# A new written order for the steps of a local attention, and the norm's bias product moved to GpSimd

## The chip, the cores and the metric

The kernel runs on one core of a Trainium2 chip. The metric is the time that the core takes for the whole kernel, in device microseconds (us). The engines are named as in the profile: PE is TensorE's matmul queue and PEld its weight loads, DVE is VectorE, ACT is ScalarE, POOL is GpSimd, SP is SyncE, which here only starts transfers.

## What is computed

The reference is a block of two layers on 16 sequences of 256 tokens with 128 features. Each layer has an attention-like part and a feed-forward-like part, each scaled and shifted per sequence (a modulation). The part that this change touches is the feed-forward place of the first layer, which is itself a small transformer of six layers with local attention in windows of 32 tokens:

```python
for i in range(DEPTH):                      # DEPTH = 6
    x = attn_layer(shift_tokens(x), Wqkv[i], q_scale[i], k_scale[i], Wo[i]) + x
    x = ffn_layer(shift_tokens(x), ln_g[i], ln_b[i], W1[i], b1[i], W2[i], b2[i]) + x

def attn_layer(x, Wqkv, qs, ksc, Wo):
    q, k, v = split(x @ Wqkv)               # 16 heads of 64
    q = l2norm(q) * qs;  k = l2norm(k) * ksc
    q = q * cos * scale + rotate_half(q) * sin * scale      # and k with 1 / scale
    out = local_attention(q, k, v)          # a window of 32 sees itself and the one before
    return out @ Wo

def ffn_layer(x, g, bln, W1, b1, W2, b2):
    mu = x.mean(-1);  var = ((x - mu) ** 2).mean(-1)
    xn = (x - mu) / sqrt(var + 1e-05) * g + bln
    a, gate = split(xn @ W1 + b1)
    return a * gelu(gate) @ W2 + b2
```

Ahead of it stands a full attention, behind it a state-space layer. Neither is changed.

## The kernel before

The kernel has three stages one after the other: `full_attention`, the class `Transformer` (the local attention), and `state_space`. `Transformer.run` handles two sequences at a time, which the code calls a group: eight groups in each of six layers, 48 in all. A group is cut into 172 small steps. Each step is a method whose name is the first letters of the step; the digits behind it say which part is meant, first the sequence of the pair (b, 0 or 1), then the half of its 256 tokens (t, 0 or 1), and where there is a third digit, a piece of the step. A `q` or `k` in the name says which of the two projections it is.

The steps of a group, with the engine of each:

- `P` (PE, line 594): projection of 128 tokens to q or k, into a two-bank tile of PSUM. `Q` (ACT, 604) squares it in two pieces, `N` (DVE, 620) multiplies it in two pieces by the sine table into `w`, `C` (DVE, 609) multiplies it by the cosine table into `u`. `R` (DVE, 631) sums the squares by head.
- `A` (POOL, 637): u + w. `MXS` (POOL, 640), `SQ` (ACT, 644) and `RR` (DVE, 647) make the reciprocal norm of the q and k of one sequence; `M` (POOL, 651) multiplies u by it.
- `T` (PE, 663): transposes of u. `E` (ACT, 679) copies them to SBUF.
- `X` (PE), `W` (ACT, 691) and `V` (SP, 696 and 697): the tokens of one sequence, and by two transfers a copy shifted by one window, in `xw`.
- `K` (ACT, 704) writes the mask into a PSUM tile, `S` (PE, 717) adds the scores to it, `MX` (DVE, 729) takes maxima, `SB` (DVE, 735) subtracts them, `EX` (ACT, 743) exponentiates, `SM` (DVE, 747 and 750) sums and inverts, `NR` (POOL, 754) scales, `TP` (DVE, 761) transposes.
- `G` (PE, 772): weights times tokens; `B` (ACT, 782) copies; `Y` (PE, 791): output product, in four pieces; `FADD` (DVE, 801) adds it to the tokens in `F`.
- The feed-forward part: `F1` (PE, 810) transposes, `F2` (DVE, 818 to 821) takes mean and variance, `F3` (POOL, 53) raises variance plus epsilon to the power -0.5, `FN` (DVE, 828) forms the bias -mean * rs, `F4` (ACT, 833) normalises, `F5` and `F6` turn it back, `FP` (PE, 863), `FE` (ACT, 867), `FM` (DVE, 873), `FY` (PE, 885) and `FF` (DVE, 898) are the two products with the gelu between them.

The string `ORDER` is the schedule. Each entry is a step and its lag: `TP11@2` means that in slot p the step `TP11` of group p - 2 is issued. `run` walks the whole list once in each slot, for 48 groups and three slots more. Every engine executes its instructions in the order in which they were issued, so the list sets the order on each engine. A slot therefore holds steps of up to four groups, and all 48 slots have the same order.

Three pools of buffers tie the engines together. The tag `two` has three PSUM tiles of two banks each; `P`, `T`, `K`/`S`, `G` (two) and `FP` all take one, 31 in each slot. The tag `one` has two single banks (`X`, `Y`, `F1`, `F5`, `FY`). In SBUF the tag `w` has four buffers, which the squares of `Q` and the products of `N` share, and `u` has seven. In the first slots of a layer `load` starts the transfers of the next layer's weights, and near its end `value_output` multiplies two weight matrices on PE.

Of the kernel before, what the change touches and what calls it, by code (L numbers as in the profile page):

```python
# [10 lines left out]
F32 = mybir.dt.float32  # L11
BF16 = mybir.dt.bfloat16
AF = mybir.ActivationFunctionType
ALU = mybir.AluOpType
# [3 lines left out]
P = 128  # L18
B, S, D = 16, 256, 128
NT = S // P  # L20
NTOK = B * S
G = 2
# [12 lines left out]
FF = int(D * 4 * 2 / 3)  # L35
# [422 lines left out]


ORDER = """  # L460
Pk01@0 Qk010@0 NR11@2 Mq00@1 TP11@2 Tq00@1 Eq00@1 Tk00@1 Aq11@1 Y03@2 Ek00@1 Aq10@1 NR10@2 Ck01@0
Nk010@0 Nk011@0 FADD0@2 TP10@2 Qk011@0 K00@1 G11@2 S00@1 MX00@1 SB00@1 FY@3 FF@3 MXS1@1 SQ1@1 B111@2
X1@1 Ak01@0 B110@2 G10@2 K01@1 RR1@1 S01@1 Mq11@1 Mq10@1 Mk10@1 EX00@1 SM00@1 MX01@1 Mk11@1 SB01@1
B100@2 Pq00@0 Rk01@0 B101@2 Qq000@0 Nq000@0 EX01@1 Pq01@0 Cq00@0 Y10@2 Qq010@0 Tq11@1 Nq001@0 Aq00@0
Y11@2 Qq011@0 Nq010@0 W1@1 Qq001@0 Cq01@0 NR00@1 Eq11@1 Nq011@0 Rq00@0 SM01@1 NR01@1 Tk11@1 Ek11@1
Rq01@0 Tk10@1 Ek10@1 Pk00@0 Ck00@0 X0@1 TP00@1 Tq10@1 Nk000@0 K11@1 S11@1 W0@1 Nk001@0 Eq10@1 MX11@1
SB11@1 Y12@2 Y13@2 V0@1 FADD1@2 Qk000@0 Qk001@0 Rk00@0 G00@1 K10@1 B000@1 S10@1 TP01@1 MXS0@0 Ak00@0
MX10@1 SB10@1 F1@2 B001@1 G01@1 Aq01@0 SQ0@0 RR0@0 B010@1 B011@1 Pk11@0 F2@2 F3@2 Pk10@0 Y00@1
EX11@1 Nk110@0 Nk111@0 FN@2 Ck11@0 Mk01@0 Ak11@0 Pq10@0 Nk100@0 Nk101@0 Qk110@0 V1@1 Ck10@0 Ak10@0
Qk111@0 Pq11@0 Mq01@0 Rk11@0 F4@2 Qk100@0 Qk101@0 Qq110@0 Qq111@0 Cq10@0 Qq100@0 Rk10@0 F5@2 EX10@1  # L470
Nq100@0 Nq110@0 Y01@1 Tk01@0 Qq101@0 F6@2 Y02@1 Nq101@0 Ek01@0 Nq111@0 Tq01@0 Eq01@0 Cq11@0 SM11@1
SM10@1 FP0@2 FE0@2 Rq11@0 FP1@2 FE1@2 Mk00@0 FM0@2 FP2@2 Rq10@0 FE2@2 FM1@2 FM2@2
"""


class Transformer:
# [335 lines left out]
    def F2(self, g):  # L812
        nc, n = self.c.nc, G * NT
        st = self.sb.tile([P, n, 6], F32, tag="fst", name="fst")
        g.mv = self.sb.tile([P, n, 2], F32, tag="fmv", name="fmv")
        g.rs = self.sb.tile([P, n], F32, tag="frs", name="frs")
        for i in range(n):
            nc.vector.bn_stats(st[:, i, :], g.f[:, i, :])
        for i in range(n):
            nc.vector.bn_aggr(g.mv[:, i, :], st[:, i, :])  # L820
        nc.vector.tensor_scalar_add(g.rs, g.mv[:, :, 1], EPS)

    def F3(self, g):
        inv_sqrt(self.c, g.rs, g.rs, [P, G * NT])

    def FN(self, g):
        g.nb = self.sb.tile([P, G * NT], F32, tag="fnb", name="fnb")
        self.c.nc.vector.scalar_tensor_tensor(g.nb, g.mv[:, :, 0], -1.0, g.rs, ALU.mult, ALU.mult)

    def F4(self, g):  # L830
        g.xn = self.sb.tile([P, G * NT, P], F32, tag="xn", name="xn", bufs=1)
# [682 lines left out]
```

## Time and profile before

| what | us |
|---|---|
| three timed runs, median (lowest to highest) | 4008.72 (4005.88 to 4009.32) |
| the profiled execution's own time | 4013.28 |
| its span, first to last instruction | 4011.4 |
| first `P` (line 594) starts | 443.1 |
| last `FF` (line 898) starts | 3452.8 |
| busy: PE, DVE, ACT, POOL | 3735.6, 3422.4, 2758.6, 2591.1 |
| mean granted TensorE clock over the span | 0.982 |

A row of the page's list of groups gives the line and engine, the operation, the output and inputs, the number of executions, the busy time and the mean duration in ns, and behind the bar the time for which the engine sat idle just before it and who ended that. In the timeline the columns are start, length, engine, line and operation, the number of instructions merged, and in square brackets the idle time before it and what ended it. In the timeline a length is that of the instruction; the next one of the same engine can start some hundredths of a us before its end.

### The profile page before, as it was taken

Reading aid. Unit: us, or ns where it says so; the run is one execution under the profiler, and the core shown is the slowest. Engines: PE = TensorE matmul, PEld = TensorE weight load, DVE = VectorE, ACT = ScalarE, POOL = GpSimd, SP = SyncE. Lnnn points to the kernel's source line nnn. Section 1 sums busy time; section 2 is a strip of 40 time slices with the busy share of each in tenths; the row PEclk is TensorE's granted clock in tenths of the full one; section 3 lists DMA queues with packets and bytes.
Section 4 is the critical chain, followed back from the end, with each engine's and each line's share of the span. In section 5 each row is a group of like instructions: output and inputs, shape, how many; then the busy total and the mean of one; then the engine's idle time right before and its main releaser. Section 6 shows DMA issues by size and latency. Waiting matters only on the chain.

```text
span 4011.4 us, 103903 instructions
## 1 busy us (share of the span) xinstructions
PE 3735.6 (93%) x45040; PEld 2202.1 (55%) x45040; DVE 3422.4 (85%) x4720; ACT 2758.6 (69%) x3962; POOL 2591.1 (65%) x1586
## 2 busy tenths in 40 slices
PE   7888789999999999999999999999999998599997
PEld 4444355555555555565655555555555555355554
DVE  4555489999999999999999999999999997299997
ACT  2555466777777777777767777677777676389995
POOL 1222477767767767767767677676676675188887
PEclk9999899999999999999999999999999999799999
DMA  0100001000010000100000000100000000134442
GB/s 24 35 7 4 1 6 34 4 7 4 6 34 4 7 7 4 34 7 4 7 10 28 7 4 6 34 4 6 7 4 7 6 4 7 53 99 114 117 110 74
DMA packets 84165, 94.42 MB, mean 24 GB/s; under 512 B 8872, under 2 KB 55804, under 8 KB 82940
## 3 DMA queue, kind: packets, MB, share of 16 engines
q1 hardware_dynamic: 83708, 87.76, 8.2%
q8 instruction: 355, 5.82, 0.6%
q14 instruction: 102, 0.84, 0.1%
HBM read 73.84 MB, written 2.62 MB: 19 GB/s over the span
## 4 chain that ended last, share of the span: by engine, by line
DVE 47%; PE 25%; POOL 11%; ACT 9%; issue 7%; DMA 0%; POOLq 0%; SPq 0%; DVEq 0%; ACTq 0%
DVE w L620 7%; DVE u L609 6%; DVE ss L631 6%; POOL u L637 6%; DVE pp L735 5%; DVE mx L729 5%; DVE sm L747 5%; PE pq L594 4%; PE y L1277 3%; PE pa L772 3%; DVE pT L761 3%; PE db L1261 2%; PE s L717 2%; ACT pp L743 2%; DVE act L873 2%
## 5 line engine op out<-in xcount | busy, mean ns | idle before, releaser
L637 POOL TENSOR_TENSOR u<-u,w 128x1024 f32<-128x1024 f32 x384 | 902.1, 2365 | 103.5 <-DVE u L609 63.0
L651 POOL TENSOR_TENSOR u<-u,r 128x1024 f32<-128x1024 f32 x384 | 722.5, 1903 | 282.7 <-DVE r L647 282.7
L594 PE MATMUL pq<-wqk,F 128*128 128x512 f32 x1536 | 731.6, 614 | 64.8 <-ACT at L782 30.8
L604 ACT ACTIVATE sq<-pq 128x512 f32<-128x512 f32 x768 | 427.7, 606 | 498.9 <-DVE w L620 258.5
L791 PE MATMUL py<-at,wvo 128*128 128x256 f32 x3072 | 743.3, 388 | 6.8 <-ACT at L782 6.3
L791 PEld LDWEIGHTS py<-at,wvo 128*128 128x128 f32 x3072 | 566.9, 191 | 132.8 <-issue 37.3
L620 DVE TENSOR_TENSOR w<-pq,sinl 128x512 f32<-128x512 f32 x768 | 493.4, 677 | 31.7 <-PE pq L594 24.0
L594 PEld LDWEIGHTS pq<-wqk,F 128*128 128x128 f32 x1536 | 275.7, 192 | 417.4 <-issue 234.0
L609 DVE TENSOR_TENSOR u<-pq,cosl 128x1024 f32<-128x1024 f32 x384 | 463.7, 1208 | 20.0 <-ACT sq L604 19.8
L631 DVE TENSOR_REDUCE ss<-sq 128x16 f32<-128x1024 f32 x384 | 459.1, 1196 | 3.3 <-ACT sq L604 1.9
L772 PE MATMUL pa<-pT,xw 32*128 32x512 f32 x3072 | 441.7, 616 | 19.9 <-ACT sq L604 16.3
L754 POOL TENSOR_TENSOR pp<-pp,sm 128x1024 f32<-128x1024 f32 x192 | 367.6, 1915 | 136.2 <-DVE sm L750 131.5
L782 ACT COPY at<-pa 128x1024 f32<-128x1024 f32 x384 | 367.9, 1010 | 52.6 <-PE pa L772 52.4
L717 PEld LDWEIGHTS s<-kT,qT 64*32 64x32 f32 x24576 | 259.6, 105 | 142.6 <-issue 77.5
L1267 DVE TENSOR_TENSOR_SCAN s<-da,db 128x512 f32<-128x512 f32 x256 | 301.1, 1207 | 24.8 <-PE db L1261 9.0
L717 PE MATMUL s<-kT,qT 64*32 64x64 f32 x24576 | 291.4, 227 | 27.3 <-ACT s L704 22.1
L729 DVE TENSOR_REDUCE mx<-s 128x16 f32<-128x1024 f32 x192 | 234.2, 1220 | 82.3 <-PE s L717 79.1
L704 ACT COPY s<-mask 128x1024 f32<-128x1024 f32 x192 | 195.3, 1017 | 155.4 <-DVE pp L735 151.8
L251 DVE TENSOR_REDUCE mx<-s 128x2 f32<-128x512 f32 x256 | 165.4, 687 | 157.8 <-PE sT L279 136.2
L663 PEld LDWEIGHTS pt<-ident,u 64*128 64x128 f32 x6144 | 217.5, 140 | 130.6 <-issue 108.4
L663 PE MATMUL pt<-ident,u 64*128 64x64 f32 x6144 | 257.8, 229 | 19.6 <-POOL u L651 6.6
L772 PEld LDWEIGHTS pa<-pT,xw 32*128 32x128 f32 x3072 | 171.6, 184 | 182.7 <-issue 105.3
(209 smaller groups left out, 6307.6 us busy)
## 6 DMA issues: line engine op xcount, KB each, us to landing
btd<-bc SPq DMA_DIRECT2D x72, 512.0 KB
bte<-bc SPq DMA_DIRECT2D x56, 256.0 KB
xw<-xw SPq DMA_DIRECT2D x96, 96.0 KB
wqk<-in_Wqk SPq DMA_DIRECT2D x6, 1024.0 KB
wv<-in_LWvT SPq DMA_DIRECT2D x6, 512.0 KB
wo<-in_Wo SPq DMA_DIRECT2D x6, 512.0 KB
xin<-in_x SPq DMA_DIRECT2D x8, 256.0 KB
out<-ot SPq DMA_DIRECT2D x8, 256.0 KB
```

Source lines behind the costliest of these rows:

```text
L594: nc.tensor.matmul(q.p[:, x], self.F[:, g.b0 + b, o : o + P], g.l.wqk[:, k, x, :], start=True, stop=True)
L604: self.c.nc.scalar.activation(q.sq[:, x], q.p[:, x], AF.Square)
L609: self.c.nc.vector.tensor_tensor(q.u.rearrange("p h x d -> p x h d"), q.p, g.l.cosl[:, t, k].unsqueeze(2).to_broadcast([P, 2, HEADS, DH // ...
L620: self.c.nc.vector.tensor_tensor(q.w[:, :, x], q.p[:, 1 - x], g.l.sinl[:, t, k, x, :].unsqueeze(1).to_broadcast([P, HEADS, DH // 2]), ALU. ...
L631: self.c.nc.vector.tensor_reduce(g.ss[b][:, t, k, :], q.sq.rearrange("p x h d -> p h x d"), AX.XY, ALU.add)
L637: self.c.nc.gpsimd.tensor_tensor(q.u, q.u, q.w, ALU.add)
L651: self.c.nc.gpsimd.tensor_tensor(uf, uf, g.r[b][:, t, k, :].unsqueeze(2).to_broadcast([P, HEADS, DH]), ALU.mult)
L663: self.c.nc.tensor.matmul(q.pt[:, r, j, :], uf[rs, j * P : (j + 1) * P], self.c.ident[rs, rs], is_transpose=True, start=(j == 0), stop=Tru ...
L717: nc.tensor.matmul(s[qs, e, j, :], qT[es, j, qs], kT[es, j, ks : ks + 2 * W], start=False, stop=True, skip_group_check=True,)
L729: self.c.nc.vector.tensor_reduce(g.mx[b, t], sf, AX.X, ALU.max)
L772: self.c.nc.tensor.matmul(g.pa[b, t, w // 2][:, w % 2, :], self.xw[b][qs, t, k, :], g.pT[b, t][qs, k, :], start=(k == 0), stop=(k == 1),)
L791: self.c.nc.tensor.matmul(g.py[b], g.l.wvo[:, h, :], self.at[:, h, :], start=(h == 0), stop=(h == HEADS - 1),)
```

## The change

`ORDER` is replaced by another list of the same steps. It starts at another point of the cycle, fifteen lags are changed (`NR10`, `NR11` and `TP10` have lag 1 and had 2; `FM1`, `FE2` and `FM2` have 3 and had 2; `X1`, `W1`, `V1` and `Y02` have 2 and had 1; `Rk10`, `Ak10`, `Tk01` and `Ek01` have 1 and had 0; `Aq11` has 0 and had 1), and the order within the slot is a new one throughout. The number of steps is the same.

The norm's bias is made in another way. `F2` makes -mean on DVE, once more a small instruction, and `FN` multiplies it by rs on GpSimd, where the power that makes rs is computed as well.

The code of the pools is not changed; which bank a tile gets follows from the order of issue.

```diff
 ORDER = """
-Pk01@0 Qk010@0 NR11@2 Mq00@1 TP11@2 Tq00@1 Eq00@1 Tk00@1 Aq11@1 Y03@2 Ek00@1 Aq10@1 NR10@2 Ck01@0
...
-SM10@1 FP0@2 FE0@2 Rq11@0 FP1@2 FE1@2 Mk00@0 FM0@2 FP2@2 Rq10@0 FE2@2 FM1@2 FM2@2
+Pq00@0 Rk10@1 Mq00@1 FM1@3 MXS1@1 Tk00@1 Ak10@1 FE2@3 FM2@3 SQ1@1 Nq000@0 Tq00@1 Nq001@0 Cq00@0
+TP11@2 Ek00@1 RR1@1 FY@3 Eq00@1 Mk11@1 FF@3 Aq10@1 K00@1 Aq00@0 Tk01@1 S00@1 Qq000@0 Mq10@1 Qq001@0
+Pk01@0 MX00@1 X1@2 Ek01@1 K01@1 Mq11@1 SB00@1 W1@2 S01@1 Nk010@0 Nk011@0 MX01@1 SB01@1 Ck01@0 V1@2
+Ak01@0 Pq01@0 EX00@1 Mk10@1 Qq010@0 Rq00@0 Y02@2 Y03@2 Qq011@0 Qk010@0 Qk011@0 G10@2 B101@2 Cq01@0
+Nq010@0 Nq011@0 X0@1 B100@2 FADD0@2 Aq01@0 G11@2 Rk01@0 SM00@1 EX01@1 B111@2 SM01@1 Pk00@0 NR00@1
+B110@2 Pq11@0 Tq10@1 Rq01@0 Qk000@0 Qk001@0 Qq110@0 Y10@2 Eq10@1 Nk000@0 Nk001@0 Ck00@0 Tk11@1 Y11@2
+Qq111@0 Nq110@0 Tq11@1 Ek11@1 Eq11@1 Tk10@1 Nq111@0 Cq11@0 TP00@1 Pk11@0 NR01@1 TP01@1 Ek10@1 Rk00@0
+Aq11@0 Y12@2 MXS0@0 Ck11@0 K11@1 S11@1 K10@1 S10@1 Nk110@0 Nk111@0 W0@1 V0@1 Ak11@0 Qk110@0 MX11@1
+SB11@1 Qk111@0 SQ0@0 MX10@1 Ak00@0 Y13@2 EX11@1 FADD1@2 G01@1 F1@2 SB10@1 B010@1 F2@2 B011@1 EX10@1
+F3@2 G00@1 B000@1 RR0@0 Rq11@0 Mq01@0 B001@1 SM11@1 Pq10@0 FN@2 Nq100@0 Pk10@0 Mk00@0 Qq100@0 SM10@1
+F4@2 Tq01@0 Nq101@0 NR10@1 Y00@1 Cq10@0 Eq01@0 Qk100@0 Rk11@0 F5@2 F6@2 Ck10@0 Qq101@0 Qk101@0 Y01@1
+Mk01@0 Rq10@0 FP0@2 FP1@2 Nk100@0 Nk101@0 FP2@2 FE0@2 NR11@1 TP10@1 FE1@2 FM0@2
 """
...
         nc.vector.tensor_scalar_add(g.rs, g.mv[:, :, 1], EPS)
+        g.nb = self.sb.tile([P, n], F32, tag="fnb", name="fnb")
+        nc.vector.tensor_scalar_mul(g.nb, g.mv[:, :, 0], -1.0)
...
     def FN(self, g):
-        g.nb = self.sb.tile([P, G * NT], F32, tag="fnb", name="fnb")
-        self.c.nc.vector.scalar_tensor_tensor(g.nb, g.mv[:, :, 0], -1.0, g.rs, ALU.mult, ALU.mult)
+        self.c.nc.gpsimd.tensor_tensor(g.nb, g.nb, g.rs, ALU.mult)
```

More of the change, by code (lines that the diff above doesn't have):

```diff
@@ L460 @@
 ORDER = """
-Pk01@0 Qk010@0 NR11@2 Mq00@1 TP11@2 Tq00@1 Eq00@1 Tk00@1 Aq11@1 Y03@2 Ek00@1 Aq10@1 NR10@2 Ck01@0
[L462 to L471, printed above, removed]
-SM10@1 FP0@2 FE0@2 Rq11@0 FP1@2 FE1@2 Mk00@0 FM0@2 FP2@2 Rq10@0 FE2@2 FM1@2 FM2@2
+Pq00@0 Rk10@1 Mq00@1 FM1@3 MXS1@1 Tk00@1 Ak10@1 FE2@3 FM2@3 SQ1@1 Nq000@0 Tq00@1 Nq001@0 Cq00@0
[10 more added lines that the diff above has]
+Mk01@0 Rq10@0 FP0@2 FP1@2 Nk100@0 Nk101@0 FP2@2 FE0@2 NR11@1 TP10@1 FE1@2 FM0@2
 """
```

## The prediction

> **What bounds the kernel now.** The page came first: its rows of busy tenths say where a stage is bound, and that the middle 30 slices are one regime.
>
> ```profile
> PE   7888789999999999999999999999999998599997
> DVE  4555489999999999999999999999999997299997
> ACT  2555466777777777777767777677777676389995
> POOL 1222477767767767767767677676676675188887
> ```
>
> From slice 6 to 33 PE and DVE are both at 9, ACT and POOL have room. The windows view puts figures to one stretch (us, then busy us of PE, PEld, DVE, ACT, POOL, then the granted clock):
>
> ```profile
> 1400.00:1800.00 400.00, 386.30 (x5588) 234.80 (x5587) 369.76 (x488) 284.22 (x373) 283.43 (x155) 1.00 0.05 13
> ```
>
> The clock is full there, so it explains nothing. Next is the timeline of DVE over one slot. The slot is a loop, so the same step comes again one period later: here `MX00`.
>
> ```profile
> 1600.37 1.22 DVE L729 TENSOR_REDUCE mx<-s 128x16 f32<-128x1024 f32 x1
> ...
> 1625.28 0.17 DVE L821 TENSOR_SCALAR frs<-fmv 128x4 f32<-128x4 f32 x1
> 1625.90 1.29 DVE L620 TENSOR_TENSOR w<-pq,sinl 128x512 f32<-128x512 f32 x2 [0.46 <-PE pq L594]
> 1627.11 1.35 DVE L828 SCALAR_TENSOR_TENSOR fnb<-fmv,frs 128x4 f32<-128x4 f32 x1
> ...
> 1650.85 1.25 DVE L761 STREAM_TRANSPOSE pT<-pp 128x1024 f32<-128x1024 f32 x1 [0.70 <-POOL pp L754]
> 1653.57 1.22 DVE L729 TENSOR_REDUCE mx<-s 128x16 f32<-128x1024 f32 x1 [1.47 <-PE s L717]
> ...
> 1656.27 1.98 DVE L898 SCALAR_TENSOR_TENSOR F<-fy,vec,F 64x256 f32<-64x256 f32 x4 [0.22 <-PE fy L885]
> ...
> 1659.56 1.22 DVE L747 TENSOR_REDUCE sm<-pp 128x16 f32<-128x1024 f32 x1 [0.72 <-ACT pp L743]
> ...
> 1661.10 1.23 DVE L729 TENSOR_REDUCE mx<-s 128x16 f32<-128x1024 f32 x1
> ```
>
> The period is 1661.10 - 1600.37 = 60.73 us. DVE waits five times in it: 0.46 + 0.70 + 1.47 + 0.22 + 0.72 = 3.57. Its work is the rest, 57.2. I check that from starts to next starts, since lengths overlap by some hundredths: 16 `N` at 0.60, 8 `C` at 1.13, 8 `R` at 1.12, 4 each of `MX` 1.25, `SB` 1.15, `SM` with its reciprocal 1.47, `TP` 1.16, then `FADD` 1.76, `F2` 1.31, two `RR` 1.0, `FN` 1.27, `FM` 1.97, `FF` 2.0: 57.1.
>
> PE in the same way, start to next start in stretches without a wait: `P` 14.0, `Y` 14.2, `G` 7.7, `S` 5.7, `T` 5.1, `FP` 5.3, `FY` 2.6, `X`, `F1` and `F5` 1.7: 56.3. So PE waits 4.4 of 60.7. POOL: 8 `A` at 2.32, 8 `M` at 1.86, 4 `NR` at 1.9, the rest 1.7: 42.8. ACT has 43 with its five table loads. Two engines have nearly the same work, and what is lost is waits of both on each other. A new order can win at most 60.7 - 56.3.
>
> Here the Trainium skill differs from the row. Its page "Perfetto Trace Analysis", section "Identifying the Most-Contended Engine", says that matmul busy time is no measure of PE's headroom and that the busy share of weight loads is one. That share is 234.8/400 = 59%; by it PE is no limit and the floor is DVE's 56. By starts PE needs 56.3. I use the starts; busy time (386.3/400 of 60.73, 58.6) would make PE the bound at 58.6, and I keep that as a rival.
>
> **The bias product.** `FN` leaves DVE: minus 1.27 a group (1627.11 to 1628.38 in the timeline above). `F2` gains one small instruction. The nearest row is its neighbour `frs`, the same kind and size, 0.17. A rule speaks against it: the page "SBUF — State Buffer", section "Who interferes with whom", says that a DVE operation with a scalar can take both ports when source and target are in SBUF, and that DVE and GpSimd then exclude each other for a whole instruction. By the rule the new instruction could wait for the power that `frs` has just released, 1.04 by its row; DVE would then save 0.1. By the row it saves 1.10. I take the row, because the new instruction is queued straight behind `frs` and starts before GpSimd can answer (the power starts 0.08 after `frs` ends). Both ends stay in the range: 0.1 to 1.1, or 5 to 52 us over 48 groups if nothing else bound.
>
> On POOL `FN` costs between 0.37 (the clamp `ss`, 128x64) and 1.04 (the power, 128x4); I take 0.6. It is queued behind one `M`. `F4` waits for it, but ACT has `Qq100` ahead of `F4`, which ends about 0.5 later than `FN` in the walk below, so it is hidden; with 1.04 it is just not late. Behind it on POOL stand `Mk00` and `NR10`; `NR10` waits for `SM10` anyway.
>
> **The order.** I read the instruction order and waits of the changed kernel, engine by engine, and walked one slot with the durations above. Each engine's order is the written one. New work is none: table loads are again two each for `SQ` and `EX` and one for `FE`.
>
> The first finding is a loop through POOL. `Nq010` takes the `w` buffer that `Ak01` reads. POOL reaches `Ak01` only after a run that begins when `RR1` ends on DVE: `Mk11`, `Aq10`, `Aq00`, `Mq10`, `Mq11`, `Ak01`.
>
> ```profile
> 1644.27 4.69 POOL L637 TENSOR_TENSOR u<-u,w 128x1024 f32<-128x1024 f32 x2
> ...
> 1658.98 3.76 POOL L651 TENSOR_TENSOR u<-u,r 128x1024 f32<-128x1024 f32 x2 [5.49 <-DVE r L647]
> ```
>
> The two POOL lines give 2.35 for an `A` and 1.88 for an `M`. The run is three of each, start to start 12.56, and with the step from `RR` to `M` (0.15) and back to DVE (0.04) 12.75. DVE has from `RR1` to `Nq010`: `FF` 2.0, `MX00` 1.25, `SB00` 1.15, two `N` 1.2, `MX01` 1.25, `SB01` 1.15, `Ck01` 1.13, `Rq00` 1.12, `Cq01` 1.13, together 11.4. So DVE waits 1.37 there, in each slot. All its other work is 56.0 - 11.4 = 44.6 (56.0 is 57.1 - 1.27 + 0.17). The loop is 44.6 + 12.75 = 57.35.
>
> The second is where PE meets it. `G11` takes the bank that `Nq011` frees; PE arrives about 1.1 early and waits. From there PE runs on: `Pk00` starts at 2.0 after `Nq011`, `Pq11` 3.7, `Y10` 6.2, `Y11` 8.6, `Pk11` 11.7, `Y12` 13.4, `S11` 15.15 to 16.75. DVE reaches `MX11` at 16.4: a wait of 0.35. `MX10`, `FADD1` and `F1` to `F2` fit within 0.15, `G00` waits 0.1 for `SB10`, `Pq10` ends 0.8 before `Nq100` wants it, `FP0` follows `F6` by 0.5, `FY` ends just as `FF` is due. Of the five waits of before, those for `P`, `EX` and `NR` are gone: `TP00` has its `NR` 5 us early, `SM00` its exponentials 9. The wait of `MX` shrinks from 1.47 to 0.35, that of `FF` to about 0.1, and 1.37 on the `w` buffer is new.
>
> Period: 57.35 + 0.35 + 0.05 = 57.75, against 60.73: 2.98 less.
>
> Moved transfers: `V0` and `V1` are two transfers each on SP. In the trace a copy `W` ends at 1611.70 and SP is through with the pair at 1613.8, so about 3 us to landing. The new order leaves 4.4 us (`V0` to `G01`) and 6.4 (`V1` to `G10`): hidden. If that cover went, PE would lose each us. The next layer's weights go to SP behind `V0`, for about 7 us, and `V1` comes over 30 later.
>
> "Banks given out by which is free first" is in no line of code: it can only have shaped the list, and is priced by the walk.
>
> **The sum.** From the first to the last `FN` lie 47 periods: 47 x 2.98 = 140. In the last layer `FF` has four more instructions of 0.48; before, those periods were 1.25 longer. Here 1.37 of DVE's wait covers them, leaving 0.56: 8 x 0.7 = 5 more. Filling and draining (147 us from the first `P` to the first `FN`, 18 after the last) I leave as they are: lags still end at 3; no row shows it, and I allow 10 either way. 4013.3 - 145 = 3868 for an execution like the profiled one, which was 4.6 above the median of the runs: **3864**.
>
> **Rivals.** (1) PE's busy time is its real need: the period stops at 58.6 to 59.5. For it: 97% busy. Against it: starts of `P`, `Y` and `FP` are even (0.43, 0.22, 0.43) and the waits between blocks visible. Time: 47 x (60.73 - 59.0) = 81, so about 3927.
> (2) The buffer wait doesn't bind, because POOL is early: PE's 56.3 and small waits give 56.9; 47 x 3.8 = 180, so 3829. Against it: three `M` and three `A` have the most even durations of all rows.
> (3) Slower: POOL's run starts late. `RR1` waits for `SQ1`, that for `MXS1`, which is queued behind `NR11` and `Mq00`. `RR1` has 3.1 of slack, the period 3.0; from 6.1 of POOL delay on, the kernel is slower, 47 us for each us. At 7.5 late: 4075. For it: POOL works off five instructions in a row there. Against it: it is idle before `Mk11` for 2.6 in my walk.
> (4) The list changes nothing, one wait for another: 4008.
>
> **Chances.** Forecast, period 57.2 to 58.4 (3840 to 3895): 0.60. Rival 1: 0.20. Rival 2: 0.07. Rival 3: 0.10. Rival 4: 0.03. Faster by over 0.2% (8 us, about what can be told from no change) is 0.87, slower 0.10. The range from 3832 to 3945 takes in the forecast, rival 1 up to 59.5 and the dearer bias product (+1.0 a group).
>
> **What would show it.** `MX00` to `MX00` near 57.75; an idle time of about 1.4 before line 620 ended by POOL u (line 637), a wait that hardly exists now; the wait of `mx` for `s` at about a quarter; `fnb` on POOL with ACT not waiting for it; DVE busy near 97%. A `fmv` multiply of over 1 us would prove the port rule; a PE wait for `xw` transfers, or ACT waiting for POOL `ss`, would make the time wrong.

## The result, and the profile after

| what | before | after |
|---|---|---|
| median of the timed runs, us | 4007.72 | 4069.38 (4066.77 to 4076.76) |
| ratio to before, 95% interval | 1 | 1.0157 (1.0139 to 1.0175) |
| span of the profiled execution, us | 4011.4 | 4065.2 |
| slot (one `F2` to the next) in the first five layers, median and mean | 60.74, 61.06 | 60.87, 61.37 |
| slots of the last layer but its last two | 61.6 to 62.0 | 60.0, then 70.3 to 73.7 |

The change made the kernel slower by 1.6%, where the forecast was 3864. The rows of busy tenths of PE and DVE on the page after:

```profile
PE   7888799999999999999999999999998888699997
DVE  4555598999998989989999889989999898289997
```

Up to slice 29 or so they look like those of before; in slices 30 to 33 (counted from 0), where the last layer of the local attention lies, PE falls from 9 to 8. The windows view of the same stretch as before (us, busy us of PE, PEld, DVE, ACT, POOL, granted clock):

```profile
1400.00:1800.00 400.00, 385.11 (x5478) 234.63 (x5477) 361.95 (x487) 284.58 (x374) 283.39 (x160) 0.99 0.05 13
```

DVE has 7.8 us less than before, since the bias product is gone, PE as much as it had. The two profiles are set side by side from `F2` of the first group to `F2` of the last: the first five layers take 10.6 us more than before, the last layer 51.6 more; the part ahead takes 7.6 less and the part behind 0.8 less. The sum is 53.8, the difference of the spans (4065.2 - 4011.4). So there are two questions: why the last layer lost so much, and why the other five gained nothing where 2.98 a slot was forecast.

**The last layer.** There `FF` has four more instructions, which put the result into `xT`. The view of one line, before and then after (minimum/median/maximum in ns):

```profile
L906 DVE SCALAR_TENSOR_TENSOR xT<-F,m0mod,xT x32: 475/481/485, 3064.1 to 3454.9; 64x256 f32<-64x256 f32 x32
```

```profile
L907 DVE SCALAR_TENSOR_TENSOR xT<-F,m0mod,xT x32: 475/2011/2598, 3056.5 to 3509.0; 64x256 f32<-64x256 f32 x32
```

The same instruction takes four times as long at the median. The timeline after, DVE and POOL in one slot of that layer, shows what stands beside it:

```profile
3198.87 2.02 DVE L899 SCALAR_TENSOR_TENSOR F<-fy,vec,F 64x256 f32<-64x256 f32 x4
3199.03 1.90 POOL L651 TENSOR_TENSOR u<-u,r 128x1024 f32<-128x1024 f32 x1 [3.27 <-DVE r L647]
3200.89 4.85 POOL L637 TENSOR_TENSOR u<-u,w 128x1024 f32<-128x1024 f32 x2
3200.93 9.17 DVE L907 SCALAR_TENSOR_TENSOR xT<-F,m0mod,xT 64x256 f32<-64x256 f32 x4
3205.69 4.13 POOL L651 TENSOR_TENSOR u<-u,r 128x1024 f32<-128x1024 f32 x2
```

The four take 9.17 us instead of 1.92 (4 x 0.481). Taken singly they last 2.59, 2.46, 2.00 and 2.01 and end 0.28 to 0.29 us behind the ends of the four GpSimd instructions of the two last POOL lines above (L637 x2, L651 x2). Both sources of line 907 lie in SBUF. The four ahead of them, line 899, are of the same operation and size, but have one source in PSUM, and keep their 0.5 each beside GpSimd's line 651. The prediction cited one rule of a section for `fmv`; here another one of that section fits: the page "SBUF — State Buffer" of the Trainium skill, section "Who interferes with whom", says that a DVE instruction with two inputs in SBUF contends with a GpSimd instruction that reads SBUF, and that the one which comes second is blocked. The new order puts `FF` right behind `RR1`, whose end starts GpSimd's run of six instructions. PE's clock followed: granted over the slots of this layer it is 0.93 (3033 to 3390 us), where before it was 1.00 (3030 to 3340).

**The other layers.** The timeline of DVE over one slot after:

```profile
1614.63 1.22 DVE L729 TENSOR_REDUCE mx<-s 128x16 f32<-128x1024 f32 x1 [0.86 <-PE s L717]
...
1618.00 1.23 DVE L729 TENSOR_REDUCE mx<-s 128x16 f32<-128x1024 f32 x1 [0.89 <-PE s L717]
1619.85 0.86 DVE L801 TENSOR_TENSOR F<-py,F 64x256 f32<-64x256 f32 x2 [0.63 <-PE py L791]
...
1622.37 0.89 DVE L818 BATCH_NORM_STATS2 fst<-f 128x6 f32<-128x128 f32 x4 [0.40 <-PE f L810]
...
1623.65 0.16 DVE L823 TENSOR_SCALAR fnb<-fmv 128x4 f32<-128x4 f32 x1
...
1656.79 1.29 DVE L620 TENSOR_TENSOR w<-pq,sinl 128x512 f32<-128x512 f32 x2 [1.14 <-POOL u L637]
```

The waits for `EX` and `NR` are gone and the one on the `w` buffer is there (1.14), as foreseen. But where a wait of 0.35 for PE was expected, a chain of four stands: 0.86 + 0.89 + 0.63 + 0.40 = 2.78. What PE did there is in its own timeline and in the list of its waits from 700 to 2900 us (total, times, longest):

```profile
1612.95 2.46 PE L717 MATMUL s<-kT,qT 64*32 64x64 f32 x204
1617.13 0.76 PE L717 MATMUL s<-kT,qT 64*32 64x64 f32 x52 [1.73 <-issue]
```

```profile
PE s L717 <- issue: 56.1, 37, 2.5
```

The scores `S11` and `S10` are 256 small matmuls (each with a weight load) without anything between them. In nearly every slot PE stops once inside them, mostly for 1.4 to 2.1 us, with nothing to wait for that the profile shows ("issue"); before, this wait was 3.1 us over all these slots, in two stops. The stop lies at another place of the 256 in each slot (204 here). On the queue of kind "instruction" 235 packets of 16,384 bytes land in these 2200 us, one for about 253 of PE's matmuls and weight loads; and each of the 37 stops ends 1.21 to 1.53 us after the end of such a packet, though these come only every 9.4 us. I read it as PE running out of instructions.

### The profile page after: what moved, and what is told of

It is laid out like the page before. It is cut to its first block, busy times and chain, and to the rows that moved or that the text cites. A ratio compares the mean times of both kernels' runs of the same rounds, so it can differ in the third digit from the quotient of the medians.

```text
span 4065.2 us, 104237 instructions
## 1 busy us (share of the span) xinstructions
PE 3732.2 (92%) x45040; PEld 2207.9 (54%) x45040; DVE 3416.0 (84%) x4720; ACT 2766.4 (68%) x3962; POOL 2601.8 (64%) x1634
## 4 chain that ended last, share of the span: by engine, by line
PE 52%; POOL 23%; issue 11%; DVE 11%; ACT 3%; DMA 0%; SPq 0%; POOLq 0%; DVEq 0%; ACTq 0%
PE py L791 11%; PE pq L594 10%; POOL u L637 9%; PE pa L772 8%; POOL u L651 8%; PE s L717 4%; POOL pp L754 3%; PE pt L663 3%; PE y L1278 3%; DVE w L620 2%; PE db L1262 2%; DVE s L1268 2%; PE fp L864 2%; PE px L1119 1%; DVE xT L907 1%
## 5 line engine op out<-in xcount | busy, mean ns | idle before, releaser
L637 POOL TENSOR_TENSOR u<-u,w 128x1024 f32<-128x1024 f32 x384 | 903.7, 2364 | 317.7 <-DVE u L609 213.8
L651 POOL TENSOR_TENSOR u<-u,r 128x1024 f32<-128x1024 f32 x384 | 730.9, 1909 | 163.5 <-DVE r L647 163.3
L594 PE MATMUL pq<-wqk,F 128*128 128x512 f32 x1536 | 748.8, 621 | 51.1 <-DVE pp L735 42.6
L791 PE MATMUL py<-at,wvo 128*128 128x256 f32 x3072 | 755.1, 392 | 8.6 <-ACT at L782 5.1
L791 PEld LDWEIGHTS py<-at,wvo 128*128 128x128 f32 x3072 | 575.6, 194 | 137.9 <-issue 51.2
L772 PE MATMUL pa<-pT,xw 32*128 32x512 f32 x3072 | 424.8, 615 | 31.9 <-DVE w L620 29.0
L1278 PE MATMUL y<-hc,ident 128*128 128x512 f32 x512 | 244.2, 604 | 16.1 <-POOL hc L1272 14.3
```

What stands on the lines that cost most here:

```text
L594: nc.tensor.matmul(q.p[:, x], self.F[:, g.b0 + b, o : o + P], g.l.wqk[:, k, x, :], start=True, stop=True)
L637: self.c.nc.gpsimd.tensor_tensor(q.u, q.u, q.w, ALU.add)
L651: self.c.nc.gpsimd.tensor_tensor(uf, uf, g.r[b][:, t, k, :].unsqueeze(2).to_broadcast([P, HEADS, DH]), ALU.mult)
L772: self.c.nc.tensor.matmul(g.pa[b, t, w // 2][:, w % 2, :], self.xw[b][qs, t, k, :], g.pT[b, t][qs, k, :], start=(k == 0), stop=(k == 1),)
L791: self.c.nc.tensor.matmul(g.py[b], g.l.wvo[:, h, :], self.at[:, h, :], start=(h == 0), stop=(h == HEADS - 1),)
```

## The experiments

Two theories followed from this. **Mine:** the lock on `xT` costs the last layer its 50 us, the stop inside `S` about 1 us a slot, and what else is missing is that PE's real need is more than the 56.3 that I had summed. **Against it:** the loop through GpSimd and the `w` buffer sets the slot, or the bias product on GpSimd costs more than it saves. All times below are medians, all ratios are to the kernel before.

**One `Y` between the two scores.** Only `Y13` is moved.

```diff
-K11@1 S11@1 K10@1 S10@1
+K11@1 S11@1 Y13@2 K10@1 S10@1
-Ak00@0 Y13@2 EX11@1
+Ak00@0 EX11@1
```

> The changed kernel with one step moved: Y13 stands between S11 and S10 in the list, so that PE no longer has 256 weight loads and 256 matmuls of S in one run. Theory (PE runs out of instructions in a double S): the idle time inside S ended by 'issue', 1.5 us a slot in the changed kernel, falls below 0.3; the wait of mx for s (92 us in all) falls; the slot goes from about 60.8 to 59.3 (58.8 to 59.9) in the first five layers, the last layer stays near 71; time about 4005 (3985 to 4025). Rival (the double S waits for its mask copy or the k copy, shown under a wrong name): the idle time stays within 0.4 of 1.5 a slot, the slot stays at 60.3 or more, time 4060 to 4080.

Measured: 4011.98, ratio 1.0013 (1.0006 to 1.002); slot 59.83 at the median (after: 60.87), the waits "PE s <- issue" 7.9 us instead of 56.1. The last layer is as slow as after (69 to 71). So the stop inside `S` was real and cost 1.04 a slot.

**The `xT` update as a step of its own.** The block under `if g.layer == DEPTH - 1:` goes from `FF` to a step `XT`, issued where GpSimd is idle.

```diff
-SQ0@0 MX10@1 Ak00@0
+SQ0@0 MX10@1 XT@3 Ak00@0
```

> The changed kernel with the last layer's update of xT taken out of FF and made a step of its own, behind MX10, where GpSimd has nothing to do. Theory (xT reads two operands from SBUF and is held by GpSimd's run of six behind RR1): one xT instruction goes from 2.0 us (median) to about 0.5, the slots of the last layer from about 71 to 62.5, time about 4012 (4000 to 4027). Rival (the last layer is slow because four more DVE instructions and the drain of lag 3 lie on the path wherever they stand): slots of the last layer stay above 68, time 4055 to 4080.

Measured: 4024.37, ratio 1.0045 (1.0029 to 1.006); slots of the last layer 61.1 to 62.5. The line of the update in this kernel:

```profile
L910 DVE SCALAR_TENSOR_TENSOR xT<-F,m0mod,xT x32: 468/480/486, 3095.0 to 3464.1; 64x256 f32<-64x256 f32 x32
```

Same data, same shapes, 0.48 again: the length hung on what GpSimd did at that time. The move alone is worth 45 us.

**The bias product alone, in either order.** In the first kernel the order is that of before and `F2` and `FN` are the new ones; in the second the other way round.

```diff
 # the order of before, with
-        self.c.nc.vector.scalar_tensor_tensor(g.nb, g.mv[:, :, 0], -1.0, g.rs, ALU.mult, ALU.mult)
+        self.c.nc.gpsimd.tensor_tensor(g.nb, g.nb, g.rs, ALU.mult)
```

> The kernel before with the old order, and the bias product alone moved to GpSimd (F2 with the extra small instruction on DVE). Theory (DVE's own work is on the path in the old order, though PE shares it): the slot goes from 60.73 to about 60.2 (59.6 to 60.5), time 3985 (3960 to 4000). Rival (the waits of PE and DVE on each other absorb it): slot 60.6 to 60.8, time 4003 to 4012. The small instruction on DVE takes 0.17 us; if the port rule held for it, 1.0.

Measured: 3979.76, ratio 0.9935 (0.992 to 0.9949), slot 60.05: about 28 us faster than before, for this edit alone.

> The new order with the bias product left on DVE as before, the reverse of the run that moved the product alone. Theory (DVE's work is on the path also in the new order): the product costs 1.0 to 1.9 us on DVE again, the slot goes from 60.9 to 61.5 or more, time about 4100 (4085 to 4140). Rival (the new order is set by PE and its instruction supply, DVE has room): slot within 0.3 of 60.9, time 4060 to 4082.

Measured: 4077.09, ratio 1.0167 (1.015 to 1.0184), slot 60.93: not told apart from the changed kernel (their intervals overlap). The line of the product on DVE, before and then in this kernel:

```profile
L828 DVE SCALAR_TENSOR_TENSOR fnb<-fmv,frs x48: 161/1344/1349, 590.0 to 3437.0; 128x4 f32<-128x4 f32 x48
```

```profile
L828 DVE SCALAR_TENSOR_TENSOR fnb<-fmv,frs x48: 99/153/164, 581.3 to 3498.6; 128x4 f32<-128x4 f32 x48
```

It works on 4 numbers a partition. The 1.34 of before were a wait for GpSimd too. In both kernels the product ends some 20 ns after GpSimd's instruction beside it (line 651) does; before, that one had 1.33 us still to run when the product began, in the new order 0.13. So at most 0.15 is left to win there.

**Both repairs, and the loop through GpSimd.** The first kernel joins the moves of `Y13` and `XT`. The second also moves `Mq11` behind `Ak01` on GpSimd, which shortens the run of six ahead of `Ak01` by one.

> The changed kernel with both edits, Y13 between the two S and xT as a step behind MX10. Theory: the gains add, slot 59.3 in the first five layers and about 61 in the last, time about 3950 (3925 to 3975), faster than the kernel before. Rivals: only one of the two causes is real, 4000 to 4030; neither, 4055 to 4080.

Measured: 3979.35, ratio 0.9934 (0.9912 to 0.9956), slot 59.71. The two repairs add up, to less than I had expected: 90 us together, 57 and 45 singly.

```diff
-K01@1 Mq11@1 SB00@1
+K01@1 SB00@1
-Ak01@0 Pq01@0 EX00@1
+Ak01@0 Mq11@1 Pq01@0 EX00@1
```

> The kernel with both edits (Y13 between the two S, xT as a step), and Mq11 moved behind Ak01, so that Ak01 comes fifth in GpSimd's run behind RR1 and not sixth. Theory (the loop RR1, GpSimd's run, Ak01, Nq010 is on the path, as the prediction put it): the wait of DVE w for POOL u, 1.0 us a slot, falls below 0.4, the wait of PE pa for DVE w of 0.7 a slot falls with it, and the slot goes from 59.7 to about 58.8, time about 3937 (3925 to 3955). Rival (PE alone sets the slot there): the wait of w goes, the slot stays at 59.4 to 59.8, time 3968 to 3985.

Measured: 3983.24, ratio 0.9937 (0.9921 to 0.9954), slot 59.57. DVE's waits for the `w` buffer over 36 slots, without and then with this move:

```profile
DVE w L620 <- POOL u L637: 35.8, 36, 1.3
```

```profile
DVE w L620 <- POOL u L637: 10.5, 37, 0.3
```

25 us of wait are gone and the time is the same. The loop was nearly as long as forecast, but it doesn't set the slot: 16 of the 25 come back as DVE's waits for ACT's squares before line 620 (2.6 to 12.6) and for PE's projection before line 609 (1.4 to 7.1), and the wait of `mx` for `s` stays as it was (77.6 and 76.6).

**Each score behind a `Y`.** On top of the second kernel's parts (`XT`, `Mq11`), with `Y13` at its old place.

```diff
-Aq11@0 Y12@2 MXS0@0 Ck11@0 K11@1 S11@1 K10@1 S10@1
+Aq11@0 MXS0@0 Ck11@0 K11@1 S11@1 Y12@2 K10@1 S10@1
```

> As the run with Ak01 early, but PE's order around the scores is S11, Y12, S10, Y13 in place of Y12, S11, Y13, S10, so that both S come one Y earlier and still apart. Theory (behind the two S stand MX11, MX10, SB10 and G00, which PE waits for 0.9 a slot): the waits of mx for s fall from 2.1 us a slot to below 1.2, G00's wait to below 0.4, at the price of up to 0.6 of PE waiting for the mask copy of S11; slot about 58.2 (57.6 to 58.8), time about 3910 (3890 to 3940). Rival (the wait for the mask eats it): slot within 0.3 of the run with Ak01 early.

Measured: 3968.51, ratio 0.9893 (0.9878 to 0.9908): the fastest kernel that does all the work, but short of what was expected. The slot is 59.70 all the same. The windows view of this kernel:

```profile
1400.00:1800.00 400.00, 392.47 (x5465) 236.14 (x5464) 366.71 (x498) 289.43 (x382) 283.91 (x164) 1.00 0.05 13
```

PE is busy for 98%, that is 58.6 of 59.7. Its listed waits, 31.6 us in the 36 slots or so, are 0.9 a slot. From start to start, summed as in the prediction, its blocks are now `P` 14.5, `Y` 14.7, `G` 9.0, `S` 5.7, `T` 4.9, `FP` 5.15, `FY` 2.77 and 1.8 of the rest: 58.5.

Not all of this is work. Two of the four `G` of a slot take 1.93 from their start to the next, the other two 2.5 to 2.65. One of these in PE's timeline, and in that of its weight loads:

```profile
1634.41 2.72 PE L772 MATMUL pa<-pT,xw 32*128 32x512 f32 x16
```

```profile
1635.14 0.73 PEld L772 LDWEIGHTS pa<-pT,xw 32*128 32x128 f32 x10 [0.43 <-ACT at L782]
```

The second half of this `G` waits until ACT has copied a tile of the `G` ahead of it (line 782) and so freed its banks. PE's own row shows no gap, because matmuls of the first half are still running. What the `G` from 700 to 2900 us take beyond 1.93 adds up to 1.3 a slot, which leaves 57.2 for PE's work.

**Half of one score left out.** In the changed kernel, `S10` makes only half of its scores, so that 192 matmuls stand together instead of 256.

```diff
-        for j in range(PAIRS):
+        for j in range(PAIRS // 2 if (b, t) == (1, 0) else PAIRS):
```

> The changed kernel with half of the scores of S10 left out (heads 8 to 15 of the first half of the second sequence keep the bare mask), all else and every wait the same. The double S then has 192 weight loads and 192 matmuls instead of 256 each. Theory (instruction supply): the idle time inside S ended by 'issue' falls from 1.5 us a slot to below 0.5, and the slot by 1.5 or more (0.7 of it is the matmuls left out), time 3990 to 4015. Rival (S10 waits for its mask or for the k copy): the idle time stays within 0.4 of 1.5, the slot falls by 0.7 at most, time 4033 to 4060.

Measured: 4005.63, ratio 0.9994 (0.9987 to 1.0001), slot 59.32. The waits inside `S`:

```profile
PE s L717 <- issue: 29.5, 23, 2.3
```

They halve (56.1 after; below 0.5 a slot was expected, it is 0.8), and there are 23 of them instead of 37. With `Y` between the scores they nearly vanish, with fewer matmuls in a row they get rarer: both fit a supply of instructions that is slower than PE's use of them in such a run. The trace has no row of PE's store of instructions; what it shows is that every long stop ends at the same short distance behind a packet of them, here too (1.19 to 1.56 us for the 21 stops of more than 0.6).

**Half of `Y`: is it PE?** PE alone loses work, 7.3 us a slot; DVE, ACT and GpSimd keep theirs. First in the fastest kernel, then in the kernel before.

```diff
-        for h in range(4 * i, 4 * i + 4):
+        for h in range(4 * i, 4 * i + 2):
-                stop=(h == HEADS - 1),
+                stop=(h == HEADS - 3),
```

> The kernel of e7_s_y_s_y with eight of the sixteen products of every Y left out (two in each piece instead of four), so the output product is over half of the heads. PE loses 32 products of 0.23 us, about 7.3 us a slot; DVE, GpSimd and ACT keep all their instructions. Theory (PE's own need, which the prediction summed to 56.3 and which is about 58.5, sets the slot of e7; the DVE and GpSimd side was summed rightly): the slot falls from 59.7 to 57.0 to 58.0, the wait of mx for s nearly goes, PE now waits, time 3968.5 less 47 x 1.7 to 2.7, that is 3840 to 3890. Rival (the DVE and GpSimd sums are short as well, by as much as PE's): the slot stays at 59.0 or more, with the waits of DVE for GpSimd and ACT grown in place of those for PE, time 3935 or more.

Measured: 3816.54, ratio 0.9521 (0.9494 to 0.9549); slot 56.29 at the median, a third of them 55.9 to 56.0. This is even below my range. In such a slot (1599.43 to 1655.37) DVE waits twice for other engines:

```profile
1609.53 0.69 DVE L620 TENSOR_TENSOR w<-pq,sinl 128x512 f32<-128x512 f32 x1 [0.18 <-POOL fnb L829]
...
1637.69 1.29 DVE L620 TENSOR_TENSOR w<-pq,sinl 128x512 f32<-128x512 f32 x2 [0.28 <-POOL u L637]
```

So DVE's own work in a slot is 55.94 - 0.46 = 55.5, where I had summed 56.0. In the new order it was PE, with its work and the waits between it, that kept the slot at 59.7. PE's busy time is no measure of that work: from 1400 to 1800 us it is 378.57 of 400 here, 53.3 of a slot of 56.29, where 58.6 less 7.3 would be 51.3. The stop inside `S` is back here too (30.7 us), with a shorter `Y12` between the scores.

> The kernel before with the same half of every Y left out. Theory (in the old order PE with its real need of about 58.5 and the waits between PE and DVE set the slot together): DVE's waits for PE (mx 1.47, w 0.46, F 0.22 a slot) mostly go and those for ACT and GpSimd (1.42) and the 1.27 of the bias product stay, slot 58.5 to 59.5, time 4008 less 47 x 1.2 to 2.2: 3905 to 3950. Rival (the old order is bound by DVE and its partners alone): slot 60.3 or more, time 3985 or more.

Measured: 4047.63, ratio 1.0098 (1.0069 to 1.0127): slower, with 7.3 us less for PE to do. Some slots are 60.74, to a hundredth the slot of before; about half are 61.58, and the rest longer still. In one of 61.58, PE's timeline and the windows around it:

```profile
1705.43 0.71 PE L663 MATMUL pt<-ident,u 64*128 64x64 f32 x16 [1.59 <-DVE w L620]
1706.18 7.11 PE L863 MATMUL fp<-hT,w 128*128 128x512 f32 x12
```

```profile
1705.00:1709.00 4.00, 3.53 (x20) 1.76 (x21) 3.96 (x6) 3.43 (x4) 1.63 (x2) 0.75 0.00 0
1709.00:1713.00 4.00, 4.00 (x9) 1.67 (x8) 3.96 (x6) 1.37 (x2) 4.00 (x3) 0.83 0.00 0
```

PE now waits longer, its granted clock falls to 0.75 and 0.83, and `FP` takes 7.11 instead of the 5.42 of a slot at full clock. The trace's record of the clock has it at one half in pieces of 3.41 us, here from 1706.98 to 1710.40. Of the 40 slots of the first five layers seven have no such piece: six take 60.73 or 60.74, and one, at the end of a layer, 62.90, as it did before. The 33 others take 61.57 or more. At full clock the old order needs the same time whether PE has this work or not. So the old order was bound by DVE and its partners ACT and GpSimd alone, and my theory of PE's share in it fell.

## Why the prediction was wrong

For the profiled execution the prediction gave a span of 3866 (4011.4 - 145); it was 4065.2, 199 us more. From the sums by layer, 130 of this lie in the first five layers (2453.4 instead of 2442.8 - 40 x 2.98 = 2323.6), 77 in the last, and -8 ahead and behind, inside the 10 that were allowed.

- **The step that failed first: the walk of PE** ("By starts PE needs 56.3. I use the starts", "From there PE runs on"). In a slot of 57.75 this leaves PE 1.45 for waits. Its work is more, and it waits where the walk had nothing. The sum took `P` and `Y` at the distances inside a block (14.0 and 14.2); from block to block they take 14.3 and 14.8 in the very slot of before. With `G` at its 7.7, which was right, PE's work is 57.2, by the sum of the fastest kernel. In the kernel after, by the list of waits, PE also loses 0.7 a slot at `G11` (25.7 us; 1.1 was foreseen), 1.56 inside `S` (56.1 us) and 0.25 elsewhere, and by the same count as in the fastest kernel 0.7 within `G`, behind ACT's copy. 57.2 + 0.7 + 1.56 + 0.25 + 0.7 = 60.4, of the 60.87 measured. Halving `Y` in the fastest kernel shows that this side holds the slot: it falls from 59.7 to 56.3 at once.
- **What the terms rest on.** The stop inside `S`, which the walk put at nothing ("`S11` 15.15 to 16.75 ... a wait of 0.35"), is shown by a run: moving `Y13` alone won 1.04 a slot. Before had it only twice in 36 slots, because there no two `S` stood together; that two came together could be read in the list. The wait within `G` is read from the trace, and no run takes it away alone.
- **Rival 1**, that PE's busy time is its need, was nearer to the slot with its 58.6, but busy time holds waits as well, as the halved `Y` shows. The share of weight loads, which the prediction weighed against it, is 59% in the fastest kernel too (236.14/400), and by it PE would have been no limit there. The list of before could have warned: its entries from 700 to 2900 add up to 75 us in 36 slots, 2.1 a slot, where my sum left 4.4.
- **The remainder.** The first five layers miss 3.25 a slot at the mean (130/40). In six of their 40 slots the clock was at one half for a piece of 3.41 us, 10.2 us lost in all, where before lost none: at most 0.25 a slot. What PE and DVE would gain if one of the other waits went is not settled.
- **The last layer**: "in the last layer `FF` has four more instructions of 0.48 ... 8 x 0.7 = 5 more". The 0.48 was right for the place of before. The lock that I weighed for `fmv` alone came here: two sources in SBUF, beside a run of GpSimd. It costs 1.5 to 2 us an instruction, 7.3 in the group shown (9.17 - 1.92). The slots grew by 8 to 12; the clock, which fell to 0.93, may have its part in that, and no run took it apart. The move of the step by itself gave 45 us back, nearly all in this layer (456.1 us from the first `F2` of the layer to the last, then 407.0; before 404.5).
- **The bias product.** The new instruction took 0.16 (0.17 by the row that I took), `FN` on GpSimd 0.20 (0.6 assumed), and `F4` didn't wait. The port rule wasn't put to the test: in none of the 48 groups did GpSimd work while the new instruction ran, since its power starts only behind it. But the 1.27 that it "leaves" was a price of its place, not of the instruction. In the old order the edit is worth 0.69 a slot and about 28 us; in the new one, nothing that can be measured. The sum counted 1.10 in full.
- **The loop through GpSimd** was right in size, a wait of 1.14 where 1.37 was forecast. Taking most of it away won nothing: it was not the longest limit.
- **DVE's work** was right (55.5 for 56.0), and so were the waits that vanish. The ceiling "60.7 - 56.3" for a new order was too high; PE's 57.2 leaves 3.5, and the best order tried won 1.0 of it.
- The forecast had its slower case at the wrong place: a late run of GpSimd. What made the kernel slower was that run standing beside DVE's `xT`, together with a gain that PE's work, its waits and the stop inside `S` had eaten.

## What to carry to other kernels

Before a new order is priced, sum the engine that comes second as carefully as the first, block by block over one whole slot rather than at the best distances between its starts, and test the sum by taking out some of its work. Its busy time is too much and its list of waits too little where a wait hides behind matmuls that still run; the row of weight loads shows such a wait. A small instruction that takes ten times its work is waiting for something beside it, so its price moves with its place; and an instruction with two sources in SBUF must be followed to what GpSimd does at its new place, also where it runs only in the last of several layers. After a list is reordered, look for equal steps that now stand side by side.

## What the runs showed of the hardware

- PE stopped, mostly for 1.4 to 2.1 us, inside 256 tiny matmuls with as many weight loads in a row, with no wait shown: 56.1 us over 36 slots, 29.5 with 192 in a row, 4.9 to 8.3 with two rows of 128 and a `Y` between them. Each of the 37 stops ended 1.21 to 1.53 us after a packet of 16,384 bytes on the instruction queue.
- A `G` of 16 matmuls took 2.5 to 2.65 us instead of 1.93 because its second half waited for ACT, without a gap in PE's row; only the row of weight loads shows 0.43 there.
- Less work on PE made a kernel slower (1.0098) because PE's clock fell in its longer waits. Over the 8 us of the two windows, 0.25 x 4 + 0.17 x 4 = 1.7 us of clock are lost, which is the 7.11 - 5.42 of `FP`. The page "TensorE: Matmul & The Clock Gate" of the Trainium skill, section "What's actually happening", tells of two states, full and half, and of a window of about 3.4 us; half speed for 3.4 us would lose just this.
- DVE instructions with two sources in SBUF grew with GpSimd beside them from 0.15 to 1.34 (`fnb`, 128x4, with GpSimd's instruction ending 0.13 and 1.33 after their start) and from 0.48 to 2.01 at the median, 2.60 at most (`xT`, 64x256).
